# A fused Swin block and dynamic convolution on TensorE: moving two convolution taps, one convolution piece, and reordering the first two steps

## The chip, the cores and the metric

One core of a Trainium2 chip. The metric is the device time of one execution in microseconds (us), lower is better. The kernel before takes 3140.25 us (median of 3 runs, 3138.6 to 3140.3). Whoever wants to save two per cent must find 62.8 us.

Names used below: PE is TensorE, DVE is VectorE, ACT is ScalarE, POOL is GpSimd. A *step* is a quarter of an image, two of its eight rows of windows (64 steps in all). A *round* is one turn of the main loop: it does the MLP of step i-2, the attention of step i and the first products of step i+1. A round is timed from its first fc1 product (`ph`) to that of the next round. In the views, `pq`, `pk` and `pe` are the qk products, `pv` those of v, `sc` the scores, `pt` and `po` the transposes and values of the attention, `pp` the projection, `pf` fc2, `st` the statistics of the norms (`st_a` to `st_c` at the start); `hid` is what a gelu writes, `dev` the variance, `win` a scaled window. *Listed idle time* is what the profile gives as idle between TensorE's records; the list of waits (`--waits`) leaves out those under 0.15 us.

## The reference

A shifted-window attention block (windows of 7x7, 6 heads, 192 channels, 56x56 pixels, 16 images) with its MLP, then a convolution whose 3x3 weights are made per image from the pooled result; the mask leaves four taps of the nine.

```python
h = _ln(h, norm1_g, norm1_b); h = jnp.roll(h, (-SHIFT, -SHIFT), axis=(1, 2)); win = ...
q, k, v = win @ qkv_w + qkv_b                      # q is scaled
attn = softmax(einsum(q, k) + bias + mask)         # bias gathered from rel_bias
x1 = shortcut + roll_back(einsum(attn, v) @ proj_w + proj_b)
y = gelu(_ln(x1, norm2_g, norm2_b) @ fc1_w + fc1_b) @ fc2_w + fc2_b
x2 = x1 + y                                        # layer 0
t = relu(gamma * (x2.mean((2, 3)) @ w1.T - running_mean) * rsqrt(running_var + EPS) + beta)
wt = (t @ w2.T + b2) * MASK                        # 4 taps left, one set per image and channel
out = depthwise_conv(x2, wt) + bias                # layer 1
```

## The kernel before

All products are float32. The kernel folds the norms' scale and mean into the weights at the start, and the norms' shifts into biases by *one-column products* (a weight matrix times one column: `qkb_p` for q, k and v, `pb_p` for the projection and fc1). PSUM is four pairs of banks, dealt out by hand; instructions of an engine run in the order in which they are written.

An image's convolution is cut into six pieces, done in the rounds of the next image: its first piece alone, then two pieces, two, and the last one. Of each piece ACT makes `y` (first tap and bias), and DVE adds three taps.

```python
def conv_rest(b, wt, n, y):                        # DVE
    ...
    tap(0, y[:, :, 1:], up[:, :, : IMG - 1])
    tap(2, y[:, :, : IMG - 1], up[:, :, 1:])
    if n in (3, 5):
        nc.vector.tensor_copy(...)                 # the border row
    tap(3, y[:, :, 1:], cur[:, :, : IMG - 1])
    conv_store(b, n, y)
# --- main loop, one round (cut) ---
cs = conv_ready(1 if convs and not convs[0]["n"] else 2)
ys = [conv_begin(*c) for c in cs[:1]]              # ACT: y of the first piece, ahead of the gelus
...
def after():
    ys.extend(conv_begin(*c) for c in cs[1:])
    for c, y in zip(cs, ys):
        conv_rest(*c, y)                           # DVE: all taps, ahead of the variance
def between():
    singles[0] = banks(f"st_{i}", C)
    keys.update(stats_of(i))
    if keys:
        var.append(norm_vars(keys))                # ACT square, DVE subtraction
# mlp_first: long ph 0..2; short ph 0..2, each with its gelu; after(); short ph 3..5; between(); long ph 3..5 with gelus
mlp_first(i - 2, yns.pop(i - 2), hid, (A, B_, C, D, A, B_), after, between)
```

The fifth fc1 group takes the bank that the first gelu reads: that is where a late gelu stops TensorE. The scores take the bank of the variance: that is where a late variance stops it.

The start, in the order of TensorE: statistics of step 0, means of wqkv, `qkb_p`, statistics of steps 1 and 2, qk and v of step 0, `pb_p`, scores of step 0, means of wf1 (`ff_m`), qk of step 1, transposes (`pt`) and values (`po`) of step 0, v of step 1, projection (`pp`), scores of step 1, qk of step 2 (with statistics `st_c` inside), `pt` and `po` of step 1, v, projection, and then the first round.

## Time and profile before

| | before |
|---|---|
| time, median | 3140.25 us |
| span of the profiled run | 3139.3 us |
| TensorE busy | 3086.4 us (98%) |
| listed idle time of TensorE, 150 to 3000 us | 10.6 us |
| first `ph` of the loop | 123.62 us |
| last engine chain | PE 84%, DVE 10% |

### The profile page before, as it was taken

How to read it: one execution, taken by the hardware profiler on the slowest of the kernel's cores; microseconds unless marked ns; L12 is line 12 of the kernel's file. 1: busy time of each engine (PE TensorE's matmuls, PEld its weight loads, DVE VectorE, ACT ScalarE, POOL GpSimd, SP SyncE). 2: the span in 40 equal slices, each digit the busy share in tenths (PEclk: the TensorE clock that was granted, in tenths of full speed). 3: DMA queues.
4: the chain of work that ended last, by engine and by line, in shares of the span. 5: the costliest groups of instructions: out<-in, count | busy, mean ns of one | idle time of the engine just before them, and what ended most of it. 6: DMA issues, size and time to landing. Idle time of an engine off the chain costs nothing.

```text
span 3139.3 us, 64443 instructions
## 1 busy us (share of the span) xinstructions
PE 3086.4 (98%) x25670; PEld 1931.8 (62%) x25670; DVE 2126.6 (68%) x3909; ACT 1881.5 (60%) x2990; POOL 1219.2 (39%) x1128
## 2 busy tenths in 40 slices
PE   8899999999999999999999999999999999999998
PEld 5566666666666666666666666666666666666654
DVE  6655766866766766766767667667667667667664
ACT  3655655656656656656556556566566566566553
POOL 4334334344344343343343343343443443433321
PEclk7999999999999999999999999999999999999999
DMA  4012121121211212121121211212112121211101
GB/s 112 18 31 62 32 75 38 40 68 44 66 37 46 64 42 70 40 62 42 48 68 35 75 37 38 72 40 65 42 45 60 46 69 38 63 44 46 35 29 54
DMA packets 98839, 160.07 MB, mean 51 GB/s; under 512 B 25718, under 2 KB 81148, under 8 KB 96620
## 3 DMA queue, kind: packets, MB, share of 16 engines
q1 hardware_dynamic: 96866, 153.62, 17.6%
q8 instruction: 203, 3.33, 0.5%
q0 software_dynamic: 1168, 1.54, 0.3%
q10 hardware_dynamic: 506, 0.79, 0.1%
q14 instruction: 96, 0.79, 0.1%
HBM read 41.26 MB, written 38.54 MB: 25 GB/s over the span
## 4 chain that ended last, share of the span: by engine, by line
PE 84%; DVE 10%; ACT 2%; issue 2%; DMA 1%; POOL 0%; ACTq 0%; SPq 0%; DVEq 0%; POOLq 0%
PE pf L92 24%; PE ph L92 16%; PE pp L92 8%; PE po L92 6%; PE pv L92 5%; PE pq L92 5%; PE pt L534 5%; PE sc L92 4%; PE pk L92 4%; PE pe L92 4%; DVE y L733 3%; PE st L92 2%; DVE vbd L477 2%; DVE x L610 1%; DVE win L357 1%
## 5 line engine op out<-in xcount | busy, mean ns | idle before, releaser
L92 PE MATMUL ph<-yn,wf 128*128 128x392 f32 (+1 forms) x3072 | 805.6, 499 | 3.9 <-ACT hid L624 3.4
L92 PE MATMUL pf<-hid,wf 128*128 128x392 f32 (+1 forms) x3072 | 802.9, 494 | 3.5 <-ACT hid L624 2.0
L521 POOL TENSOR_TENSOR prob<-e,tot 113x588 f32<-113x588 f32 x256 | 297.7, 1174 | 1156.2 <-DVE tot L520 1150.0
L92 PEld LDWEIGHTS ph<-yn,wf 128*128 128x128 f32 (+1 forms) x3072 | 422.8, 188 | 358.5 <-issue 78.7
L477 ACT COPY vbd<-pv 49x192 f32<-49x192 f32 x512 | 160.1, 313 | 693.3 <-DVE vbd L477 688.7
L92 PEld LDWEIGHTS pf<-hid,wf 128*128 128x128 f32 (+1 forms) x3072 | 386.5, 164 | 303.6 <-issue 119.8
L670 DVE SCALAR_TENSOR_TENSOR x<-pf,cols,x 128x784 f32<-128x784 f32 (+1 forms) x128 | 106.1, 829 | 531.1 <-PE pf L92 495.6
L624 ACT ACTIVATE hid<-ph,f1b 128x784 f32<-128x784 f32 x384 | 336.9, 913 | 102.7 <-PE ph L92 101.3
L263 POOL TENSOR_TENSOR sq<-sq,sq 64x392 f32<-64x392 f32 x252 | 259.3, 1029 | 281.2 <-ACT sq L257 267.7
L274 POOL TENSOR_TENSOR xs<-x,x 64x392 f32<-64x392 f32 x246 | 248.9, 1012 | 234.9 <-DVE x L610 225.6
L733 DVE SCALAR_TENSOR_TENSOR y<-x,wt,y 128x770 f32<-128x770 f32 x282 | 321.0, 1148 | 16.6 <-ACT y L726 8.1
L92 PEld LDWEIGHTS pv<-wqkv,win 64*128 64x128 f32 (+1 forms) x2048 | 255.7, 189 | 31.5 <-issue 1.2
L92 PE MATMUL pv<-wqkv,win 64*128 64x192 f32 (+1 forms) x2048 | 272.7, 326 | 0.5 <-ACT kbd L431 0.5
L512 DVE TENSOR_TENSOR e<-e,top 113x588 f32<-113x588 f32 x256 | 264.8, 1034 | 8.9
L92 PE MATMUL pp<-o,wp 128*128 128x392 f32 (+2 forms) x896 | 251.4, 514 | 0.0
L505 DVE TENSOR_TENSOR e<-sc,bias_t 113x588 f32<-113x588 f32 x256 | 179.3, 762 | 106.3 <-PE sc L92 106.2
L540 ACT COPY prt<-pt 128x678 f32<-128x678 f32 x256 | 179.2, 726 | 119.4 <-PE pt L534 117.9
L245 ACT ACT_TABLE_LOAD x193 | 247.6, 1283 | 5.2 <-issue 1.8
L515 ACT ACTIVATE e<-e 113x588 f32<-113x588 f32 x256 | 176.8, 691 | 116.3 <-DVE e L512 116.3
L534 PEld LDWEIGHTS pt<-ident,prob 113*128 113x128 f32 x1536 | 166.9, 142 | 72.2 <-issue 39.8
L92 PE MATMUL po<-prt,vbd 128*64 128x49 f32 x6144 | 199.2, 225 | 4.3 <-ACT kbd L431 4.3
L477 DVE COPY vbd<-pv 49x192 f32<-49x192 f32 x512 | 181.3, 354 | 31.7 <-PE pv L92 24.5
(167 smaller groups left out, 4077.0 us busy)
## 6 DMA issues: line engine op xcount, KB each, us to landing
dv<-dev SPq DMA_DIRECT2D x1012, 49.0 KB
xs<-x SPq DMA_DIRECT2D x246, 98.0 KB
x<-in_x_dram SPq DMA_DIRECT2D x15, 1484.0 KB
out_dram<-y SPq DMA_DIRECT2D x48, 392.0 KB
out_dram<-y SPq DMA_DIRECT2D x48, 196.0 KB
x<-in_x_dram SPq DMA_DIRECT2D x16, 392.0 KB
x<-in_x_dram SPq DMA_DIRECT2D x15, 350.0 KB
out_dram<-y SPq DMA_DIRECT2D x16, 308.0 KB
```

What stands on the lines that cost most here:

```text
L92: nc.tensor.matmul(dst, lhs, rhs, start=start, stop=stop, skip_group_check=True)
L245: nc.scalar.activation(junk, eps_t[0:1], func)
L263: (adder or nc.gpsimd).tensor_tensor(s0[p, h], s0[p, h], s1[p], ALU.add)
L274: nc.gpsimd.tensor_tensor(s0[p, h], v0[p, h], v1[p], ALU.add)
L477: copy(dst, src[s * 64 : s * 64 + N, h, :, :, j, :])
L505: nc.vector.tensor_tensor(e, sc[:PW, :, : HEADS * N], rel, ALU.add)
L512: nc.vector.tensor_tensor(ehs[wp], ehs[wp], t.broadcast_to([PW, 2 * HEADS, N]), ALU.subtract)
L521: nc.gpsimd.tensor_tensor(prob[wp][:PW, :, 0:N], ehs[wp], t.broadcast_to([PW, 2 * HEADS, N]), ALU.mult)
L534: nc.tensor.transpose(pt[:, a, g * PW : (g + 1) * PW], prob[wp][:PW, h : h + 2, :].rearrange("p h k -> p (h k)"), ident[:PW, :PW],)
L540: nc.scalar.copy(prt, pt[:, :, : 3 * PW])
L624: nc.scalar.activation(hid[:, f], phs[f][:, :, :T], AF.Gelu, bias=f1b[:, f : f + 1])
L733: nc.vector.scalar_tensor_tensor(dst, src, wt[:, kc, t : t + 1], dst, ALU.mult, ALU.add)
```

## The change

Three parts. (A) In rounds with two pieces, two taps of the second piece go behind the variance. (B) In the round with an image's first piece, `y` goes behind three gelus. (C) The start: loads of the relative bias go from the sync queue to POOL's, clearings from DVE to POOL, the bias tables are built in pieces at idle moments of DVE, the second parameter transpose goes ahead of the means of wqkv, the scores of step 0 ahead of `pb_p`, the scores of step 1 ahead of its v and of the projection, `ff_m` from ahead of qk of step 1 to behind that projection, and the statistics `st_c` from within qk of step 2 to ahead of it. The window scaling of step 2 goes from DVE to POOL, and one table load of ACT is saved. No matmul is added or taken away.

```diff
-    def conv_rest(b, wt, n, y):
+    def conv_rest(b, wt, n, y, part=None):
...
-        tap(0, y[:, :, 1:], up[:, :, : IMG - 1])
+        if part != 1:
+            tap(0, y[:, :, 1:], up[:, :, : IMG - 1])
+        if part == 0:
+            return
         tap(2, y[:, :, : IMG - 1], up[:, :, 1:])
...
-        cs = conv_ready(1 if convs and not convs[0]["n"] else 2)
-        ys = [conv_begin(*c) for c in cs[:1]]
+        first = bool(convs) and not convs[0]["n"]
+        cs = conv_ready(1 if first else 2)
+        ys = [] if first else [conv_begin(*c) for c in cs[:1]]
...
-            ys.extend(conv_begin(*c) for c in cs[1:])
-            for c, y in zip(cs, ys):
-                conv_rest(*c, y)
+            ys.extend(conv_begin(*c) for c in cs[len(ys) :])
+            for k, (c, y) in enumerate(zip(cs, ys)):
+                conv_rest(*c, y, 0 if k else None)
...                                     # in between(), behind norm_vars:
+            for c, y in zip(cs[1:], ys[1:]):
+                conv_rest(*c, y, 1)
```

The start, cut to the lines that the argument touches:

```diff
+            nc.gpsimd.dma_start(rel_r[q : q + WS]..., ...)      # 14 of them, was nc.sync, later
...
-    nc.vector.memset(kbd, 0.0)
-    g2, be2, f2b, pb, cb = columns(*rows3, 1)
+    add(nc.vector)                                             # adds of the squares of step 1
...
-    norm1_scale(0, dvs.pop(0), nc.vector)
+    biases(0, 0)
     for dst, c, at, _, n, b in parts: ...                      # qkb
+    norm1_scale(0, dvs.pop(0), nc.vector)
+    nc.gpsimd.memset(kbd, 0.0)
...
+    top, share = attention_scores(0, *qs.pop(0), (0, 2, 3, 1))  # now ahead of pb_p
-    pv = banks("pb_p", 3)
+    pv = banks("pb_p", 0)
...
-    pm = fold_means(wf1, HID, "ff", 0)                         # was ahead of qk of step 1
     qs[1], outs = attention_qk(1, 2, 3, 1)
...
+    top, share = attention_scores(1, *qs.pop(1), (0, 3, 2, 1))
     pvs, v_rest, v_whole = attention_v(1, (0, 3))
     pp, pair1, p_narrow, p_rest, p_whole = project(0, o, 2, 1)
+    pm = fold_means(wf1, HID, "ff", 0)
+    norm_stats(keys, {0: 3, 1: 0})                             # st_c, was inside qk of step 2
     qs[2], outs = attention_qk(2, 2, 0, 1)
```

## The prediction

> **What bounds the kernel now.** I read the page first, then the waits of TensorE over the whole run and by stretch, then busy time by window, then the timelines of all engines at the start and in a round that convolves.
>
> ```profile
> PE 3086.4 (98%) x25670; PEld 1931.8 (62%) x25670; DVE 2126.6 (68%) x3909; ACT 1881.5 (60%) x2990; POOL 1219.2 (39%) x1128
> PEclk7999999999999999999999999999999999999999
> ```
>
> TensorE is busy for 3086.4 of 3139.3 us; only 52.9 us of it are idle. The change keeps the number and shapes of the matmuls, so it can win back only idle time and time in which matmuls ran at a lowered clock. The second line shows that lowering in the first of the forty slices only. The windows say where the idle time lies:
>
> ```profile
> 0.00:20.00 20.00, 10.13 (x23) 3.02 (x23) 10.85 (x32) 4.37 (x8) 11.69 (x22) 0.84 0.85 216
> 40.00:60.00 20.00, 18.95 (x155) 14.17 (x154) 16.06 (x44) 5.39 (x13) 12.35 (x23) 0.61 0.77 195
> 80.00:100.00 20.00, 13.99 (x156) 7.45 (x155) 17.86 (x37) 10.61 (x19) 4.38 (x4) 0.97 0.01 2
> 100.00:120.00 20.00, 13.62 (x148) 12.66 (x150) 4.95 (x9) 11.00 (x18) 14.64 (x18) 0.69 0.22 51
> 400.00:2800.00 2400.00, 2390.51 (x20078) 1500.74 (x20076) 1664.99 (x3038) 1474.87 (x2344) 952.29 (x857) 1.00 0.19 53
> ```
>
> The third number is TensorE's busy time, the third from the end the granted clock. The first 120 us hold 25.4 us of idle time (9.9, 1.3, 1.0, 0.8, 6.0 and 6.4 in the six windows); 200 to 3000 us hold 10.6; the last 139 us hold 16.7. The waits of TensorE, first up to 150 us, then from 150 to 3000 us:
>
> ```profile
> PE cols_p L146 <- DVE cols_rows L143: 4.8, 1, 4.8
> PE po L92 <- ACT kbd L431: 4.3, 1, 4.3
> PE cols_p L146 <- DMA cols_rows<-in_L_conv_qkv_b_dram: 4.2, 1, 4.2
> PE pt L534 <- ACT q L412: 4.1, 1, 4.1
> PE pt L534 <- POOL prob L521: 2.7, 1, 2.7
> ...
> PE sc L92 <- DVE dev L310: 5.5, 16, 0.4
> PE ph L92 <- ACT hid L624: 3.4, 15, 0.2
> ```
>
> Columns: total, times, longest. So the steady rounds lose 8.9 us in 31 small waits, and the start five large ones. Last, the timeline of TensorE:
>
> ```profile
> 20.67 0.27 PE L146 MATMUL cols_p<-ident,cols_rows 5*128 5x5 f32 x1 [4.83 <-DVE cols_rows L143]
> 54.41 5.74 PE L92 MATMUL ff_m<-wf,ones 128*128 128x384 f32 x7
> 102.12 3.63 PE L534 MATMUL pt<-ident,prob 113*128 113x113 f32 x18 [2.74 <-POOL prob L521]
> 110.02 5.36 PE L92 MATMUL po<-prt,vbd 128*64 128x49 f32 x96 [4.27 <-ACT kbd L431]
> 123.62 1.55 PE L92 MATMUL ph<-yn,wf 128*128 128x392 f32 x4
> ```
>
> The reader should keep 123.62: the first fc1 product of the first round of the loop. All that the change does to the start is in when this instruction comes. The same 96 po products take 3.03 us at full clock (at 70.03) and 5.36 here: the waits before them lowered the clock too.
>
> **What the Trainium skill says.** "TensorE: Matmul & The Clock Gate", Part 1, says that the clock halves after an idle window of some 3.4 us and comes back after a busy one, the windows running free. The trace agrees: in 3 us windows the clock falls to 0.50 after the gap at 13 us, after the gaps at 94 to 102 and at 106 to 110, and also during the one-column products of 41.6 to 48.3 us, which count as busy here but evidently not for the clock. "GPSIMD Engine Reference", 3.1, puts two-input elementwise work on GpSimd at 1.96 times VectorE's time; here the window scaling of one step takes 3.14 us on DVE (22.23 to 25.37) and 5.71 on POOL (46.26 to 51.97), 1.8 times. "DMA: Bandwidth & Descriptors", section on the SWDGE path, gives a fixed cost of about 2 us; the small parameter rows issued by POOL here land after 5.0 to 5.5 us, the queues being full. That is the figure I use for the loads moved to POOL.
>
> **The change, part by part.** *Steady rounds.* (a) In a round with two pieces, three taps of each (some 1.1 us) stand on DVE ahead of the variance. In the rounds with the extra border copy the variance comes late, and the scores, which reuse its bank, wait: 16 times, 5.5 us in all. With two taps (2.2 us) behind it the variance is held only by ACT's square of the mean (ends about 418.7 us in the round at 413 us) and ends near 419.9, the products ahead of the scores near 421.4. The two taps then end near 422.0, just when the first score tile is there, so the bias adds start no later. 5.5 us go. (b) An image's first piece: y (1.03 us at 317.82) stands before three gelus, so the first gelu ends at 319.78 and the product reusing its bank starts at 319.84 after 0.23 us. Behind them, y ends near 321.3, and DVE reaches the taps at 321.88 anyway: 3.4 us go, nothing is added. I count 8.5 of 8.9.
>
> *Start, first half.* Several things go ahead of the first step. The second parameter transpose no longer waits behind the 2.02 us clearing of kbd (which goes to POOL, 2.2 us by its 0.97 us for 1024 columns): the 4.8 us wait goes. Its rows land near 12.7 us (issued 7.15, plus 5.5), DVE copies them near 13.4, and the column means of wqkv stand behind it, 13.9 to 18 instead of 11.9 to 15.6. Then qkb_p 4.95, to 23; statistics 4.4, to 27.3; DVE finishes 1.15 of adds, 1.4 of biases, 0.9 of small sums and 3.14 of scaling near 27.3. The first pq comes near 27.4, not 29.8. No pk wait; qk takes 6.6, v 4.3: to 38.3 (41.6 before). Now the scores come ahead of the 6.8 us of pb_p, whose time covers the softmax. With two short waits for evictions they end near 42.4 and pb_p near 49.2. The qk of step 1 then starts in a lowered clock, 9.5 us for a warm 6.7, to 59; transposes 3, po 3: to 65 (73.0 before, but there with the 6.3 us of ff_m done).
>
> *Start, second half.* Scores of step 1 with some 1.1 us waiting for the copy of po: 67.7. v 4.4 and projection 3.9: 76.0. ff_m, now warm, 2.6: 78.6. Next the statistics of step 3 and step 0, which were hidden among qk products and now stand ahead of them: residual on DVE to 79.4, squares on ACT to 80.8, their adds on POOL to 82.9. That is 2.8 us of new waits. qk of step 2 meets the subtraction of the ff_m bank, which stands on DVE behind the softmax (86.0): 1.8 more. It ends at 92. But by now the softmax is through, and ACT goes from its root straight to gelu without the second exp load (1.28). The 4.1 and 2.7 us waits at the transposes go, and the 4.3 at po shrinks to 0.4: po ends near 98 instead of 115.4. v waits 0.2 for e (ACT 98.9), ends at 102.2; projection to 106.1. So ph comes near 106.5 against 123.62: 17.1 us.
>
> *Cross-check.* Before: 25.4 idle, and about 11 lost to the clock (ff_m 3.5, po 2.3, v 1.5, the rest in smaller pieces). After: about 15.5 idle (4.3 + 2.9 + 0.6 at the start, 1.6 in scores, 1.1, then 4.6, under 1 at the end of it) and 6 lost to the clock. That gives 15. I take 16. The tail is untouched.
>
> Sum: 16 + 8.5 = 24.5; 3140.25 - 24.5 = 3115.75, rounded to 3116.
>
> **Rivals.** (1) The waits only change names: the first half is bound by the chain residual, squares, statistics and by DVE's long list, and moving clearings, scaling and fourteen loads to POOL, the slower engine, makes POOL late. For it: POOL gets 7.4 us of issues ahead of its squares, so they end near 21.6, not 18.9; the loads of the relative bias end only near 20 to 22 us, and DVE's first bias add stands ahead of the scaling. Against: the statistics ask for those squares only near 25.4. It would leave 8 us of the 16: 3124. (2) The steady part gives back what it takes: the two taps delay the bias adds, qk then waits for its banks. For: DVE has work nearly without a gap there; against: it idles 1.92 us before the bias adds in the round at 328 us. Gain 3 or less: 3121. (3) The clock stays up through the start: pb_p is followed by dense products, and without the waits at 94 to 110 nothing lowers it. Gain at the start 21: 3111. (4) No time moves, transfers bind: against, the queues are idle from 60 us on.
>
> **Range and chances.** The start is 16 with an error of some 7, from one chain worked by hand; the phase of the clock's window can shift some 2 us; the steady part is 8.5 with an error of 2. Together 3108 to 3126. 2% are 62.8 us, more than all the idle time of TensorE, so faster by over 2% is nearly ruled out, and slower would take a new 1 us wait in every round.
>
> **What would show it.** In the changed profile: DVE dev and ACT hid gone from TensorE's waits between 150 and 3000 us, with at most 2 us idle there; the first ph of the loop at 102 to 113 us; no cols_p wait above 1 us on the second transpose; new waits of st_c on POOL sq and of pe on the wf subtraction, 1 to 3 us each; ff_m under 3.5 us; clock still lowered near 50 us. I would be wrong if ph comes after 115, or if a new wait recurs in every image's rounds.

## More of the kernel before

The prediction shows the views. One line it doesn't show is the chain that ended last, by engine: in the kernel before a tenth of it runs over DVE.

```profile
PE 84%; DVE 10%; ACT 2%; issue 2%; DMA 1%; POOL 0%; ACTq 0%; SPq 0%; DVEq 0%; POOLq 0%
```

## The result, and the profile after

| | before | after |
|---|---|---|
| time, median of 4 runs on one chip | 3139.82 us (3138.6 to 3140.3) | 3107.81 us (3107.48 to 3110.14) |
| ratio | | 0.99 (0.9883 to 0.9917) |
| span of the profiled run | 3139.3 us | 3105.7 us |
| first `ph` of the loop | 123.62 us | 110.16 us |
| from there to the first `ph` of the last round | 2966.0 us | 2945.0 us |
| rest | 49.6 us | 50.6 us |

A ratio is the mean time of one kernel's runs over that of the other's of the same rounds, so not quite the ratio of the medians quoted. Executions over 1.5% slower than the fastest of the same kernel are left out of the means. The change gains 32.0 us by the medians, 1%, so "within 2%". By the profiled spans it is some 33.5: 13.5 at the start, 21.0 in the rounds, and 0.9 given back at the end.

The page after, part 1 and the row of the granted clock, then the chain by engine:

```profile
PE 3073.1 (99%) x25670; PEld 1927.8 (62%) x25670; DVE 2118.6 (68%) x3893; ACT 1880.4 (61%) x2989; POOL 1245.4 (40%) x1165
PEclk8999999999999999999999999999999999999999
...
PE 96%; DVE 2%; DMA 1%; ACT 0%; issue 0%; POOL 0%; POOLq 0%; DVEq 0%; ACTq 0%
```

TensorE's busy time fell by 13.3 us, though it does the same 25670 products: what looks busy was partly waiting or slow. The chain is now TensorE alone. The windows of the start and of the long middle stretch (third number TensorE's busy time, third from the end the granted clock):

```profile
0.00:20.00 20.00, 11.74 (x26) 4.16 (x26) 8.62 (x31) 5.40 (x10) 15.12 (x31) 0.89 0.86 212
80.00:100.00 20.00, 17.35 (x110) 8.84 (x110) 14.03 (x22) 14.26 (x23) 14.53 (x25) 1.00 0.17 41
100.00:120.00 20.00, 20.00 (x171) 12.47 (x168) 11.71 (x33) 10.29 (x21) 10.95 (x11) 1.00 0.09 21
400.00:2800.00 2400.00, 2399.82 (x20323) 1511.53 (x20320) 1672.76 (x3045) 1487.06 (x2359) 961.05 (x865) 1.00 0.19 53
```

Idle time from 400 to 2800 us fell from 9.49 to 0.18 us, and from 80 to 120 us the clock is full and 2.65 us are idle (12.39 before). The waits of TensorE, up to 150 us and then from 150 to 3000 us (total, times, longest):

```profile
PE cols_p L146 <- DMA cols_rows<-in_L_conv_qkv_b_dram: 4.5, 1, 4.5
PE pq L92 <- DVE win L363: 2.3, 1, 2.3
PE cols_p L146 <- DVE cols_rows L143: 2.2, 1, 2.2
...
PE pe L92 <- DVE wf L177: 1.0, 1, 1.0
PE st_c L92 <- POOL sq L266: 0.9, 2, 0.7
...
PE sc L92 <- DVE dev L316: 0.2, 1, 0.2
```

Of the 31 waits in the rounds one of 0.2 us is left; of the 4.1, 2.7 and 4.3 us waits at `pt` and `po` one of 0.4 is left at `po`. The longest wait that remains, 4.5 us for the first parameters, was there before (4.2). And the timeline of TensorE, with the lines that answer to those of the prediction:

```profile
79.18 3.33 PE L92 MATMUL ff_m<-wf,ones 128*128 128x384 f32 x8
95.16 3.34 PE L540 MATMUL pt<-ident,prob 113*128 113x113 f32 x24
99.31 2.77 PE L92 MATMUL po<-prt,vbd 128*64 128x49 f32 x88 [0.44 <-ACT prt L546]
110.16 2.14 PE L92 MATMUL ph<-yn,wf 128*128 128x392 f32 x6
```

So far everything is as it was meant to be, but the rounds gave 21.0 us where only 10.4 us of listed idle time (10.6 before, 0.2 after, from 150 to 3000 us) were there to be won. Round by round (in the traces, first `ph` to first `ph`), the gain lies in the rounds that the change touches:

| kind of round | before | after | listed idle before |
|---|---|---|---|
| image's first piece (15 rounds) | 47.80 us | 47.02 us | 0.23 us |
| two pieces, first time (14) | 47.31 | 47.09 | 0.14; 12 of the 14 are too short for the list of waits |
| two pieces with border copy (14) | 47.53 | 47.09 | 0.37 |
| last piece (14) | 47.54 | 47.54 | 0 |

The last image's rounds fall where the loop runs empty: its first piece lost as much (47.12 against 46.36 us), its rounds with two pieces are the same in both kernels (40.27 and 26.93 us).

The loop's first round gained 0.5 us too (47.54 to 47.02); rounds that convolve nothing are at 47.02 in both kernels. Each of the three kinds lost more than is listed: 0.78, 0.22 and 0.44 us. The single records of the first kind of round show where. A fc1 product's record lasts 489 to 493 ns, but in a dense stretch the next one starts after 323 to 330 ns; the last 166 ns overlap. (The starts are measured; the profile models the ends of matmuls.) When TensorE stops, the loss starts at the missed issue (323 ns), while the listed idle time starts at the end of the record (489 ns): the first 166 ns of this wait are not listed. The product behind the stop lasts 593 ns, its successors start after 427, 365 and 427 ns, not 323, and the statistics behind them take 135 ns more (1589, not 1454):

```profile
319.84 1.73 PE L92 MATMUL ph<-yn,wf 64*128 64x392 f32 x8 [0.23 <-ACT hid L624]
321.50 1.00 PE L92 MATMUL st<-xs,sel 128*32 128x392 f32 x8
```

0.229 listed + 0.166 + 0.104 + 0.042 + 0.104 + 0.135 = 0.78 us. That is a reckoning from the records of one round; the experiment with the doses below tests its sum, not each term.

### The profile page after: what moved, and what is told of

Its sections match the earlier page's. It is cut to its first block, busy times and chain, and to the rows that moved or that the text cites.

```text
span 3105.7 us, 64444 instructions
## 1 busy us (share of the span) xinstructions
PE 3073.1 (99%) x25670; PEld 1927.8 (62%) x25670; DVE 2118.6 (68%) x3893; ACT 1880.4 (61%) x2989; POOL 1245.4 (40%) x1165
## 3 DMA queue, kind: packets, MB, share of 16 engines
q8 instruction: 203, 3.33, 0.5%
## 4 chain that ended last, share of the span: by engine, by line
PE 96%; DVE 2%; DMA 1%; ACT 0%; issue 0%; POOL 0%; POOLq 0%; DVEq 0%; ACTq 0%
PE ph L92 25%; PE pf L92 24%; PE pv L92 8%; PE pp L92 8%; PE po L92 6%; PE pq L92 5%; PE pt L540 5%; PE sc L92 4%; PE pk L92 4%; PE pe L92 4%; PE st L92 3%; PE pc L92 0%; DMA rel_r<-in_L_conv_rel_bias_dram 0%; DVE vbd L483 0%; DVE e L518 0%
## 5 line engine op out<-in xcount | busy, mean ns | idle before, releaser
L92 PEld LDWEIGHTS po<-prt,vbd 128*64 128x64 f32 x6144 | 188.9, 138 | 9.7 <-ACT prt L546 0.6
```

Of the source, the lines that this page charges most:

```text
L92: nc.tensor.matmul(dst, lhs, rhs, start=start, stop=stop, skip_group_check=True)
```

## The experiments

"Before" is the kernel before, run in the same rounds on the same chip: its medians were 3140.67, 3140.65, 3141.21 and 3140.76 us. All kernels gave correct results.

### A and B: one part of the change alone

A is the kernel before with the two taps moved, B with the first piece moved (the parts of the diff above).

> The kernel before with one part of the change alone: two taps of a round's second piece behind the variance. Theory H (a late bank costs more than the idle time that the profile lists for it): the two kinds of rounds with two pieces become 0.22 and 0.44 us shorter, in 15 images, 9.9 us in all, about 3130. Rival P (the prediction: the listed waits are the loss): 5.5 us, about 3134.5. Rival S (the rounds became shorter because the new start shifted the engines against each other): nothing, 3140.

> The kernel before with one part alone: an image's first convolution piece behind three gelus. Theory H: 0.78 us in each of 15 rounds, 11.7 us, about 3128. Rival P: the listed 3.4 us, about 3136.5. Rival S: nothing.

A: 3131.49 us (3130.67 to 3133.04, 5 runs), ratio 0.9971 (0.9957 to 0.9985): 9.2 us less. In its trace the rounds take 2956.96 us, 9.1 less; two-piece rounds are at 47.10, first-piece rounds still at 47.80. B: 3128.84 us (3128.02 to 3131.72, 5 runs), ratio 0.9963 (0.9951 to 0.9976): 11.8 us less; rounds 2955.03 us, 11.0 less; first-piece rounds at 47.02, the others as before but for one at 48.35, which lost 0.8 us at another place (a wait of 0.33 at `pe`). The waits of TensorE from 150 to 3000 us, of A and then of B, show that each part takes away its own wait and leaves the other's:

```profile
PE ph L92 <- ACT hid L624: 3.4, 15, 0.2
```

```profile
PE sc L92 <- DVE dev L310: 5.3, 15, 0.4
```

A removed 5.5 us of waits from the list and won 9.1; B removed 3.4 and won 11.0. Both are near theory H (9.9 and 11.7) and far from rival P (5.5 and 3.4); rival S, that the new start did it, is out.

### C: the start alone

The kernel after with both parts in the rounds undone (the diff of A and B the other way round).

> The changed kernel with both steady parts undone, so the new start alone. Theory H: 13.5 us less than before (the first fc1 product at 110.2 instead of 123.6 us), about 3126.5, and rounds as long as before. Rival P: 16 us, about 3124. Rival S: 24 us or more, about 3116, with shorter rounds.

3129.98 us (3129.17 to 3131.4, 5 runs), ratio 0.9966 (0.9953 to 0.9978): 10.7 us less, not the 13.5 of theory H. First `ph` at 112.45 us, rounds 2965.19 us, 0.8 less than in the kernel before, most of it in the loop's first round. A, B and C add up to 31.7 us; the whole change gave 32.0. The parts don't help or hinder each other. The start differs by some 2 us from profile to profile of the same code: the first `ph` came at 123.62, 123.10 and 125.30 us with the old start (before, A, B), at 110.16, 112.45 and 112.21 with the new one (after, C and the doses below). By these means the start gains 12.4 us, not 13.5.

### Doses: what a wait of a given length costs

The kernel after, but in each round with an image's first piece a growing part of `y`, then dummy activations too, goes back ahead of the gelus.

```diff
+DOSES = [(0, 0), (3, 0), (6, 0), (8, 0), (10, 0), (12, 0), (14, 0), (14, 1), (14, 2), (14, 3), (14, 4), (14, 0), (10, 0), (6, 0), (0, 0), (0, 0)]
...
+            rows, extra = DOSES[cs[0][0]]
+            if rows:
+                ys = [conv_begin(*cs[0], None, 0, rows)]
+            for _ in range(extra):
+                nc.scalar.activation(idle, ones[:, 0:64], AF.Identity)
```

> The kernel after, but in the rounds with an image's first piece (every fourth round) a growing piece of y goes back ahead of the first gelu (0, 3, 6, 8, 10, 12, 14 of 14 rows), then 14 rows and 1 to 4 small dummy activations (some 0.2 us each) as well, then 14, 10, 6, 0 rows again as a repeat; the rest of y stays behind the gelus. Read round by round in the one trace: period of the round minus 47.02 us (the loss) against the idle time that is listed ahead of the fifth fc1 product. Theory (part of a wait hides behind the overlap of two matmuls, and the first matmul after a stall is slower): no loss at few rows, then a loss that is some 0.5 us larger than the listed idle time, at every dose, and some doses with a loss and nothing listed: 14 rows lose 0.78 with 0.23 listed, and each further dummy adds its own 0.2 to both. Rival (the prediction's reading: a wait costs what is listed): the loss equals the listed time within 0.05 us at every dose, and the 0.78 of the kernel before came from something else in that round.

One run of 3120.13 us (state unknown, as it is a single run; read within its own trace only). Per round, from the records (the period without a dose is 47.02 us):

| ahead of the first gelu | y part, us | listed idle, us | loss, us | loss less listed |
|---|---|---|---|---|
| 3 rows | 0.51 | 0 | 0.58 (0.27 by the end of fc1) | |
| 6 rows (twice) | 0.66 | 0 | 0.40, 0.41 | |
| 8 rows | 0.76 | 0 | 0.50 | |
| 10 rows (twice) | 0.84 | 0.04, 0.04 | 0.58, 0.59 | 0.54, 0.55 |
| 12 rows | 0.93 | 0.14 | 0.69 | 0.55 |
| 14 rows (twice) | 1.03 | 0.23, 0.23 | 0.78, 0.78 | 0.55, 0.55 |
| 14 rows and 1 dummy | | 0.37 | 0.93 | 0.56 |
| and 2, 3, 4 dummies | | 0.66, 0.94, 1.24 | 1.21, 1.50, 1.79 | 0.55, 0.56, 0.55 |

Two of these rounds in the timeline of TensorE, with 14 rows and with 14 rows and 4 dummies:

```profile
1443.27 1.73 PE L93 MATMUL ph<-yn,wf 64*128 64x392 f32 x8 [0.23 <-ACT hid L632]
...
2203.73 1.73 PE L93 MATMUL ph<-yn,wf 64*128 64x392 f32 x8 [1.24 <-ACT hid L632]
```

The theory holds at every dose from 10 rows on: a wait at this place costs the listed time and 0.55 us, and the group behind the stop takes 1.73 us whether the stop was short or long. The rival, that a wait costs what is listed, is out. With 6 and 8 rows nothing at all is listed, and 0.40 and 0.50 us are lost. Where the loss begins was not found: "no loss at few rows" did not come true. The 3-row round lost 0.27 us in the fc1 stretch and 0.31 more later, among the qk products; that one round was not explained. At the scores no doses were tried; there 0.14 us of idle time cost 0.22, and 0.37 cost 0.44.

### D: the first window earlier

In the kernel after, the first qk product comes at 30.87 us, 3.5 us later than predicted. VectorE stands behind two slow adds, beside the squares on POOL, which begin late because of POOL's fourteen loads. D gives half of the loads back and moves a group of bias adds.

```diff
-            nc.gpsimd.dma_start(
+            (nc.gpsimd, nc.sync)[j].dma_start(
...
-    biases(0, 0)                 # ahead of the qkb sums
...
     norm1_scale(0, dvs.pop(0), nc.vector)
+    biases(0, 0)
```

> The changed kernel; half of the fourteen relative-bias loads go back from POOL's queue to the sync queue, and the first six bias sums stand behind the window scaling of step 0 instead of ahead. If POOL's late squares (20.65 us, beside DVE's adds, which took 3.73 instead of 1.15 us) and the bias sums make the first pq late: POOL's squares near 14 us, DVE's adds 1.2 us, the first pq near 28 instead of 30.9, the first fc1 product near 107.5, some 2.5 us less in all. Rival: what follows (evictions on ACT, the spread of the next step) sets the start anyway: the gain is lost before the first fc1 product, 0 us.

3108.33 us (3107.36 to 3109.0, 4 runs), ratio 0.9896 (0.9883 to 0.991): no better than the kernel after; the first `ph` came at 111.71 us, not 107.5. The rival held. The timeline of DVE shows the adds, in the kernel after and then in D:

```profile
20.95 3.73 DVE L266 TENSOR_TENSOR sq<-sq,sq 64x392 f32<-64x392 f32 x2
```

```profile
21.91 1.15 DVE L266 TENSOR_TENSOR sq<-sq,sq 64x392 f32<-64x392 f32 x2
```

Two adds take 3.73 us beside POOL's squares and adds, and 1.15 without them. The Trainium skill, "SBUF — State Buffer", section "Who interferes with whom", says that a VectorE instruction with two SBUF inputs contends with a GpSimd instruction that reads SBUF, since the second input comes through the read interface that the two share. The trace agrees: the first add lasts 2.43 us, not some 0.6, and ends 0.43 us after POOL's two squares; the second, beside POOL's own adds, lasts 1.27. But the 2.6 us are not what the time hangs on: D's first qk product comes at 30.18 us, yet `pb_p` begins at 45.51 us in both kernels. In D VectorE's list (bias adds, reciprocal, scaling of wf1) reaches the copies of v at 40.48 us without a gap; in the kernel after it is through 0.72 us earlier and the copies begin at 40.48 us too, when TensorE releases them. Behind that D is no earlier, and its `pb_p` and qk of step 1 end 1.56 us later than in the kernel after (62.81 and 61.25 us), as more of them ran in the lowered clock.

### F: the means of wf1 ahead of qk of step 1

In the kernel after, `ff_m` stands behind the projection. F puts it back ahead of qk of step 1 (and gives `pb_p` another pair of banks).

```diff
+    pm = fold_means(wf1, HID, "ff", 0)
     qs[1], outs = attention_qk(1, 2, 3, 1)
...
     share(3)
+    fold_center(wf1, HID, pm)
```

> The kernel after with the column means of wf1 (ff_m, 3.3 us there) ahead of the qk products of step 1, so in the lowered clock, and their subtraction early on VectorE. Theory (the lowered clock lasts for a stretch of time that the one-column products and the dense work behind them set, whatever runs in it): no loss, -1 us (0 to -1.5), since the wait of pe on the wf subtraction (1.0) goes. Rival (the prediction's reckoning, in which what runs in the lowered clock costs twice and what is moved out of it is won): ff_m takes near 6 us again and the run is about 3 us longer.

3113.73 us (3112.23 to 3114.71, 5 runs), ratio 0.9914 (0.9901 to 0.9928): 26.9 us less than before, so 5.1 of the 32.0 are lost. My theory fell; the rival's direction was right and its size too small. The timeline of TensorE in F:

```profile
53.59 5.74 PE L92 MATMUL ff_m<-wf,ones 128*128 128x384 f32 x7
85.56 0.85 PE L92 MATMUL st_c<-x,sel 128*32 128x392 f32 x4 [1.08 <-ACT vbd L483]
87.43 2.83 PE L92 MATMUL st_c<-x,sel 128*32 128x392 f32 x11 [1.01 <-DVE x L616]
```

In the lowered clock `ff_m` holds TensorE for 5.55 us (53.59 to 59.15, when the qk products have it to themselves), at full clock 3.26 (79.18 to 82.44 in the kernel after). The other half of the loss is cover: without `ff_m` behind the projection the statistics wait for the copies of v and for the residual, 2.1 us in two pieces, and the clock falls there (0.91 from 80 to 100 us). The first `ph` comes at 114.60 us.

### G: the one-column products ahead of the scores again

```diff
-    top, share = attention_scores(0, *qs.pop(0), (0, 2, 3, 1))
     pv = banks("pb_p", 0)
     ...                          # the pb_p products
+    top, share = attention_scores(0, *qs.pop(0), (2, 3, 1, 0))
```

G also moves the adds of `pb` and `f1b` up and gives the transposes of w1 (`w1p`) a bank of their own, at which TensorE now waits 1.1 us. No run separates that from the order, but it lies ahead of a longer wait for the same softmax.

> The kernel after with the one-column products (pb_p) back ahead of the first step's scores. Theory (behind the scores their 8 us cover the softmax): the gain of that is lost, about 2 us longer (1 to 4), as a wait of the transposes on POOL prob. Rival (the order of these two does not matter, as the same products are done by the same time): within 0.5 us of the kernel after, and no new wait over 1 us.

3112.13 us (3110.43 to 3113.13, 4 runs), ratio 0.9908 (0.9895 to 0.9922): 28.5 us less than before, 3.5 of the 32.0 are lost. The theory held. The waits of TensorE from 25 to 125 us:

```profile
PE pt L540 <- ACT q L418: 4.0, 1, 4.0
...
PE pt L540 <- ACT prt L546: 1.2, 2, 1.1
```

The releaser differs from what I had written (ACT's eviction of q, which stands behind the exponentials, not POOL), but it is the softmax of step 0 that is not covered: its last exponential starts at 60.58 us, the eviction at 61.30, the transposes at 62.35.

### H: one-column products in the idle time before the first qk product

Half of the fc1 shifts (12 of 24 one-column products) go into the 2.34 us in which TensorE waits for the first window.

```diff
     norm_stats(keys, {0: 1, 1: 2})
+    for f in range(3):
+        shift(pqf[:, 1, f : f + 1], rawf, f * 128, 128, be2)
+    nc.vector.tensor_copy(f1c, pqf[:, 1, 0:3])
...
-    for f in range(NFC):
+    for f in range(3, NFC):
         shift(pv[:, 1, f : f + 1], rawf, f * 128, 128, be2)
```

> The kernel after with half of the f1b products (12 of the 24 one-column products, 3.1 of their 6.2 us) moved into the 2.34 us in which TensorE waits for the first scaled window of step 0. Theory (the wait is TensorE's to fill, and the softmax of step 0 has slack to spare): the first qk product comes 0.5 to 1 us later, pb_p takes 3 us less, net -2 us (-3 to -1). Rival (the softmax needs the cover): the transposes of step 0 wait for POOL prob by 1 to 2 us, and the time is within 0.5 us of the kernel after.

3107.26 us (3106.12 to 3108.88, 4 runs), ratio 0.9894 (0.988 to 0.9907): not to be told from the kernel after. Neither expectation's reason held: `pt` doesn't wait for POOL, and yet the 2 us didn't come. The windows of 4 us show why, first H and then the kernel after:

```profile
32.00:36.00 4.00, 4.00 (x15) 3.52 (x16) 2.99 (x10) 1.65 (x2) 1.70 (x3) 0.50 0.02 4
```

```profile
32.00:36.00 4.00, 4.00 (x17) 2.31 (x14) 4.00 (x9) 3.02 (x4) 1.08 (x2) 1.00 0.02 4
```

In H the clock is at 0.50 until 36 us, and qk of step 0 takes 9.2 us (32.35 to 41.55) instead of 6.4 (30.87 to 37.30). The three microseconds taken from `pb_p` were paid there.

### I, J, K and L: do one-column products lower the clock?

I is the kernel after with each `pb_p` product taking its column 64 times over; J is H with all one-column products, those of `qkb_p` too, so widened; K is F with `pb_p` so widened; L is G with 128 columns (with other banks and adds to hold them).

```diff
+    def wide(col):
+        return col.broadcast_to([col.shape[0], 64])       # 128 in L
...
-        mm(dst, raw[:, 0, lo : lo + n], be[0], True, False)
+        mm(dst, raw[:, 0, lo : lo + n], wide(be[0]), True, False)
```

> The kernel after, in which each of the 36 one-column products (pb_p) takes its column 64 times over (a broadcast operand), so that TensorE streams 64 columns and not one; one of the 64 equal result columns is read. Nothing else changes. Theory (products of one column do not hold the granted clock up, though TensorE counts as busy): the clock stays at 1.00 from 44 to 60 us, pb_p takes at most 7 us (8.0 there), qk of step 1 6.7 (7.9 there), and the first ph comes 2 to 3 us earlier: about 3105.5. Rival (the two short waits among the scores, or the phase of the clock's windows, lower the clock): it is lowered as before, pb_p is as long or longer, and the time is within 1 us of the kernel after or above it.

> h_fill (half of the f1b products in the wait for the first scaled window) with all one-column products, those of qkb_p too, widened to 64 columns. Theory (h_fill won nothing since one-column products held the clock at 0.50 up to 36 us, so that the qk of step 0 took 9.2 us and not 6.4): the clock is up by 31 us, qk of step 0 takes 6.4 to 7, the gain of the filling appears, first ph 3 to 5 us earlier than in the kernel after, until the softmax of step 0 limits it: about 3104. Rival (the softmax of step 0 bounds the stretch, whatever TensorE does): transposes of step 0 wait 2 to 4 us, and the time is within 1 us of the kernel after.

> f_means_early with the one-column products widened as in i_wide. Theory (ff_m ahead of qk of step 1 cost 5 us because it ran in the lowered clock): ff_m takes 3.3 us, not 5.5, and the run is within 1.5 us of i_wide, so about 3106. Rival (it cost because of the waits that follow it, of st_c on ACT vbd and DVE x, 2.1 us in two pieces, and the clock lowered behind them): those waits stay, and the run is 2 to 4 us longer than i_wide.

> g_pb_first (pb_p ahead of the first step's scores, so directly behind dense products and with no wait ahead of it) with each of the 36 one-column products widened to 128 columns. In g_pb_first the clock falls near 46 us, 4 us into these products, though TensorE has had no idle time since 29.84 us. Theory (products whose time is spent on loading weights, with the array streaming only a small part of it, lower the clock; 64 columns of some 53 ns in a step of 180 ns were too few in i_wide): with 128 columns it stays at 1.00 from 36 to 49 us, the scores behind take 2.6 us and not 3.5. The run's time stays that of g_pb_first (3112) within 1.5 us, since the softmax of step 0 bounds what follows. Rival (the width does not matter): the clock falls to 0.50 to 0.65 between 46 and 50 us again.

| | median, us | ratio (95%) | first `ph`, us |
|---|---|---|---|
| I | 3108.03 (3106.97 to 3109.26, 4 runs) | 0.9896 (0.9883 to 0.991) | 111.78 |
| J | 3108.48 (3107.33 to 3108.93, 4 runs) | 0.9897 (0.9883 to 0.991) | 110.33 |
| K | 3114.31 (3110.14 to 3116.2, 5 runs) | 0.9914 (0.99 to 0.9927) | 117.19 |
| L | 3111.56 (3109.89 to 3112.4, 4 runs) | 0.9906 (0.989 to 0.9923) | 115.22 |

None is faster than the kernel after. I: the clock falls all the same, only later (0.50 from 52 us), and the rival held in the time. J: the clock is up from 30 us on, qk of step 0 takes 6.5 us again, but the clock falls behind the scores as in the kernel after, POOL's scaling of step 1 is waited for by 0.78 us, and the time does not move: theory half right, no gain. K: `ff_m` still ran in the lowered clock (56.62 to 62.15), which 64 columns did not hold up; so K tells nothing of its theory, and the waits of the rival are there.

G and L are the clean pair: `pb_p` follows dense products with no wait ahead of it, and only the width differs. The products, then windows of 2 us, G and then L (in G the scores follow from 47.24 us on, so its second window holds them alone):

```profile
43.24 4.07 PE L92 MATMUL pb_p<-cols,raw 128*128 128x1 f32 x24
...
46.00:48.00 2.00, 2.00 (x28) 1.94 (x31) 0.00 (x0) 0.00 (x0) 1.93 (x3) 0.63 1.07 174
48.00:50.00 2.00, 2.00 (x57) 2.00 (x54) 1.09 (x3) 0.00 (x0) 1.77 (x7) 0.51 0.97 170
```

```profile
45.30 5.07 PE L92 MATMUL pb_p<-cols,raw 128*128 128x128 f32 x24
...
46.00:48.00 2.00, 2.00 (x11) 1.40 (x11) 0.00 (x0) 0.40 (x2) 2.00 (x3) 1.00 1.01 253
48.00:50.00 2.00, 2.00 (x11) 1.40 (x11) 0.00 (x0) 0.00 (x0) 1.85 (x4) 1.00 1.05 189
```

TensorE is busy for 2.00 of 2.00 us in all four; with one column the clock falls (to 0.50 from 46.5 to 50.0 us), with 128 it stays at 1.00 through all 7.2 us of them (43.12 to 50.37), and the scores behind take 2.25 us and not 3.53. The theory held: it is the width of the products, with no wait involved. Each is a single trace, so the clock's phase could have helped, but the others speak against it: in all 13 other traces (three of them with 64 columns), wherever `pb_p` stood, the clock fell 0.2 to 4.7 us after its first product, and in the kernel before, A and B `pb_p` also followed dense products with no wait just ahead, and the clock fell after 2.4 to 4.7 us. As an estimate, a column of the dense products takes 323 / 392 = 0.82 ns, so 128 columns fill 105 ns of L's 211 ns per product (5.07 us for 24), 64 columns 53 ns of the 182 that I's take at full clock: half was enough. That under a third is not enough isn't shown as cleanly, since in I, J and K 1.3 us of waits among the scores stand just ahead of `pb_p`. What lies between was not tried. No time was won, since the softmax of step 0 bounds what follows (`pt` waits 4.0 us in L as in G).

No version beats the kernel after by more than the scatter; H's median is 0.6 us below it, within the range of its own runs.

## Why the prediction was right, and where its working was not

**The verdict and the mechanism were right.** Within 2% was all but certain, as TensorE's idle time, 52.9 us, is less than that. The waits it named went, but for one of 0.2 us, and no new one recurs; the first `ph` at 110.16 us lies in its 102 to 113. All the other marks of "what would show it" hold but two: the second transpose still waits 2.2 us (`cols_p`, "no wait above 1 us" was said), and `st_c` waits 0.9 us, just under the 1 to 3 given.

**The sum was too small: 24.5 us were predicted, 32.0 came.** The median, 3107.81 us, lies 0.2 us below the range's low end. Two terms were mis-sized, in opposite directions.

*The steady rounds, 8.5 us.* This is the step that failed, and by more than the whole miss: "5.5 us go" was 9.1 (A), and "3.4 us go, nothing is added" was 11.0 (B); together 21.0 in the trace after, 0.5 of them in the loop's first round. The causes, the moves and the places were right; the size was read from the list of waits as if the list were the loss. The doses show what it leaves out: 0.55 us for each stop at the fifth fc1 product (15 x 0.55 = 8.3 us; B won 8.4 beyond its listed 3.4 by the medians, 7.6 in its trace). At the scores the loss was 0.44 for 0.37 listed, and the 14 rounds in which 0.14 us were idle, 12 of them not in the list at all, lost 0.22 each (3.1 us). (So the 16 waits that the prediction put down to the rounds with the border copy are 14 of these and 2 of the others.) The number that should have warned was in the trace of the kernel before and on a page cited anyway: the Trainium skill, "TensorE: Matmul & The Clock Gate", Part 2, "Single matmul latency", gives one bf16 product a fixed part of about 166 ns at full clock on top of its streaming time. The trace's records agree (489 ns each, 323 ns from one to the next), but as their ends are modelled this is no independent measurement; what a stop costs is shown by the doses. A better reading would have been the period of each kind of round, not its idle time: before, 47.80, 47.31 and 47.53 us against the 47.02 us of the rounds that convolve nothing. The range's error of 2 us on this term was far too narrow.

*The start, 16 us.* It gave 13.5 in the two profiles and 12.4 by the means of three each. The chain, point by point:

| | predicted, us | after, us |
|---|---|---|
| first qk product | 27.4 | 30.87 |
| scores of step 0 end | 42.4 | 45.5 |
| `pb_p` ends | 49.2 | 53.3 |
| qk of step 1 ends | 59 | 61.3 |
| scores of step 1 end | 67.7 | 71.1 |
| `ff_m` ends | 78.6 | 82.4 |
| qk of step 2 ends | 92 | 95.2 |
| first `ph` | 106.5 | 110.16 |

The lag of some 3.5 us is there at the first qk product and is there at the end (it is 2.3 to 4.1 between). It arose in "DVE finishes 1.15 of adds, 1.4 of biases": the adds took 3.73 and the biases 2.08 us (1.47 in D), beside POOL's work. Rival (1) had seen POOL late (squares near 21.6 us, measured 22.95) and set it aside since the statistics ask later; it missed that VectorE's adds, which stand ahead of the window scaling, are slowed beside them. Yet D shows that undoing this in part wins nothing: its first qk product is 0.7 us earlier, but VectorE reaches the copies of v at 40.48 us as before. So "the first pq comes near 27.4" failed on VectorE's list, which was too long for it in either order.

The other terms behind it err in both directions: `pb_p` 7.8 us (6.8 said), since more of it ran in the lowered clock; qk of step 1 7.9 (9.5); the new waits of `st_c` and `pe` 1.9 (4.6); `ff_m` 3.33, against the bound of 3.5 and 2.6 in the sum. F confirms that moving `ff_m` out of the lowered clock is worth something (2.3 us, and as much again for the cover it gives), G that the order of scores and `pb_p` is worth 3.5.

The cross-check came nearer than the 16 taken: of the idle time up to 120 us, 25.4, it left 15.5 and the windows after show 16.1; that leaves 4.1 of the 13.5 for the clock, where it had 5. One of its readings of the clock was wrong: there is no gap "at 13 us". TensorE is busy from 11.89 to 15.64 us in the kernel before, and the clock falls at 13.5 in the midst of it, 1.6 us after a gap of 1.2; the gap of 4.8 us comes later.

*The rivals.* (2), that the steady part is given back, is refuted by A and B; (3), that the clock stays up, by the windows (0.50 from 48 to 56 us in the kernel after); (4), that no time moves, by the result. (1) came true in its first half only.

**What stays open.** Why the end is 0.9 us longer with the new start (50.6 us, in C too; 49.6 before). It lies behind the work of VectorE, which ends 42.96 us after the last round's first `ph` in both: the last store is issued at 45.50 and 45.82 us from there, and SyncE is through at 48.68 and 49.73. Open too are the 0.31 us of the 3-row round, and which width up to 128 columns holds the clock up.

## What to carry to other kernels

Where an engine is 98% busy, don't price a small recurring wait by its listed idle time: take the period of the rounds with it and without it. Here 31 listed waits of 8.9 us, with 12 too short for the list, were worth 20.5 us. A product that streams one column is dear twice, for its own time (155 ns in G at full clock, against 211 for 128 columns in L) and for the clock it leaves to what follows. Before filling an idle stretch or moving work forward, ask what that work covers where it stands, and on which engine's list the next release hangs.

## What the Trainium skill lacked or had wrong

- "TensorE: Matmul & The Clock Gate", Part 1, ties the clock to how busy TensorE is and warns of idle windows. It lacks that products of few columns lower it with no idle time at all: 2.00 of 2.00 us busy and clock 0.63, then 0.51, with one column (G); 1.00 with 128 columns (L); 0.50 from 52 us on with 64 (I, with short waits ahead).
- The same page, Part 2, "Single matmul latency", has the 166 ns (here 489 ns a record, 323 ns from start to start), and "Perfetto Trace Analysis" says that the end of a TensorE record is an estimate; neither says what follows for reading waits: the first 166 ns of one are not listed as idle, and a stop at the tiled fc1 products costs 0.55 us more than is listed (0.78 for 0.23, 1.79 for 1.24).
- "SBUF — State Buffer", "Who interferes with whom", agrees with the runs; nothing was wrong there. What it cost was to be measured: two adds that take 1.15 us together took 3.73 beside GpSimd's squares and adds.
- "DMA: Bandwidth & Descriptors", the section on the SWDGE path, gives some 2 us of fixed cost, and no figure for queues that are full; the small rows issued by GpSimd at the start landed after 5.0 to 5.5 us in the kernel before, with full queues.
